# Attention with a gated feed-forward: block 0's row exps in one instruction, a sigmoid by exp and log, and the softmax statistics turned earlier

## The chip, the cores and the metric

The kernel runs on one core of a Trainium2 chip. A core has a matrix engine (TensorE, PE in the profile; PEld is its weight load), a vector engine (VectorE, DVE), a scalar engine for functions like exp (ScalarE, ACT), a general engine (GpSimd, POOL) and a queue for transfers (SyncE, SP). Each engine works through its own list of instructions in order; semaphores make one wait for another. The metric is the device time of the kernel in microseconds (us), the median of several runs.

## The reference

The input x has 16 batches of 512 rows of 128 numbers, all float32. Cut to what matters:

```
xn = layernorm(x)
q, k = xn @ Wq, xn @ Wk          # 16 heads of 8
v = xn @ Wv                      # 16 heads of 64
attn = softmax(causal(q k^T / sqrt(8)))      # 512 x 512 for each head
a = (attn @ v) @ Wo
prev = xn moved down by one row, a row of zeros first
xr, xk = mu_r*xn + (1-mu_r)*prev, mu_k*xn + (1-mu_k)*prev
f = sigmoid(xr @ W_r^T) * (relu(xk @ W_k^T)^2 @ W_v^T)
out = x + a + f
```

## The kernel before

**Two passes over the scores.** For a softmax row one needs its maximum and the sum of its exps. The kernel computes the scores twice. The first pass has queries on the partitions: PE writes them to a PSUM tile `sm` (`rowscores`), adds the causal mask by further small products (`rowmask`), DVE takes each row's negated maximum `negm` (`rowmax`), and ACT takes exps with `negm` as bias and sums them along the row into `z` (`rowsum`). The log of `z` (`log_sums`, ACT) is subtracted from `negm` (`sub_logs`, DVE); the result `lz` is the number that turns a score into the log of its weight. `turn_stats` transposes `lz` on PE (tile `pm`) and DVE splits it into a high and a low part (`mh`, `ml`); `put_stats` sends these by four DMAs, issued by POOL, into two extra rows of the query tile `q`. The second pass has keys on the partitions: `scores` (PE, tile `sT`) multiplies with the extra rows, so that the exp of its result is the finished weight. `weights` (ACT) takes that exp into `e`, POOL zeroes what lies above the diagonal, and `weigh` (PE, tile `av`) multiplies with `v`. `take_ctx` (DVE) copies the sum out as `ctx`, and `project_out` (PE, tile `po`) applies Wo.

**Tiling.** Heads are taken in pairs, one head on partitions 0 to 63 and one on 64 to 127, and two pairs make a group. A row block is 128 queries; block i has (i+1) x 128 keys at or below the diagonal. A group's blocks are packed into five tiles, `ROWS` for the first pass and `KEYS` for the second. A unit handles one tile of each. In `ROWS`, tiles 0 and 2 hold block 2 (384 keys) and block 0 (128 keys) of one pair, tiles 1 and 3 hold block 3 (512), and tile 4 holds block 1 (256) of both pairs. A batch is four groups, so 20 units, and unit n of kind t = n mod 5.

**Order.** The order of the work is written out by hand: `_InOrder` keeps every engine's instructions in the order of the program. `unit_work(n)` issues, for unit n, the first pass's row scores and masks for the tile that is 11 units ahead, the second pass's scores for tile n, any turn of statistics that is due, `take_ctx`, the maxima of the tile 11 ahead, the row exps of the tile 10 ahead (`LEAD`), the weights of tile n, and then the pieces and the weighted values. The pieces are the rest of the work (normalising, projections, the feed-forward part), put into units by `at(n, ...)`; they come before the weighted values, and in units of kind 1 after them. A group's log of sums is taken in a unit of kind 4; `sub_logs` is appended to the pieces of the next unit, the turn comes one unit after that, and the sending one more after.

**Buffers.** `sm` has two buffers of two PSUM banks, `sT` one of two banks, `av` one bank, and one bank `m` is shared by all pieces (`m_tile`), `pm` included. So row scores wait for ACT's row exps two tiles back, and scores wait for the last unit's weights.

**Feed-forward.** `ffn_r` makes the argument of the sigmoid in tile `pr`; DVE copies it with a lower clamp into `e_sig`, ACT takes exp(-x) (`ffn_exp`), POOL adds 1, and DVE's reciprocals in four parts give `sig` (`ffn_sig`). `ffn_out` multiplies with it.

**Transfers.** `project_qk` writes q and k of a later batch to DRAM and `spread_qk` (SP) reads them back in the layout of the pairs, in 16 transfers per batch at written-out units.

Of the kernel before, what the change touches and what calls it, by code (L numbers as in the profile page):

```python
# [17 lines left out]
P = 128  # L18
# [7 lines left out]
LEAD = 10  # L26
EPS = 1e-5
MASKED = -3.0e38
SIG_MIN = -87.5


class _InOrder:
# [15 lines left out]
def attn_ffn_kernel(  # L48
# [119 lines left out]
    def product_turned(out, lhsT, rhs, start=True, stop=True):  # L168


        for t in range(NB):
            for c in range(2):
                first = t * P + 64 * c
                pe.matmul(
                    out[64 * c : 64 * c + 64, t * D : (t + 1) * D], lhsT[:, first : first + 64],
                    rhs, start=(start and t == 0), stop=(stop and t == NB - 1),
                )
# [85 lines left out]
    def ffn_r(b):  # L263
        pr = m_tile(f"pr_{b}")
        product_turned(pr, xmix.pop((b, 0)), ffn_w[:, 0, :])
        e = one.tile([P, T], FP, tag="e_sig", name=f"e_sig_{b}")

        dve.tensor_scalar(e, pr, SIG_MIN, None, ALU.max)
        ffns[b, "e"] = e

    def ffn_exp(b):
        e = ffns[b, "e"]
        act.activation(e, e, AF.Exp, scale=-1.0)
        pool.tensor_scalar(e, e, 1.0, None, ALU.add)

    def ffn_sig(b, c):
        if c == 0:
            ffns[b] = one.tile([P, T], FP, tag="sig", name=f"sig_{b}")
        cols = slice(c * P, (c + 1) * P)
        dve.reciprocal(ffns[b][:, cols], ffns[b, "e"][:, cols])  # L280

    def ffn_k(b):
        pk = m_tile(f"pk_{b}")
# [57 lines left out]
    def rowmask(b, g, t):  # L341

        ends = [to + (i + 1) * P for _, i, to in ROWS[t]]
        step = ends[-1] - ends[0] or P
        for c in range(2):
            for u in range(2):
                s = slice(64 * u, 64 * u + 64)
                cols = sms[b, g, t][:, u, ends[0] - P :]
                if len(ends) > 1 and step > P:
                    cols = cols.rearrange("q (m k) -> q m k", k=P)[:, 0 :: step // P, 64 * c :]  # L350
                else:
                    cols = cols.rearrange("q (m k) -> q m k", k=P)[:, :, 64 * c :]
                pe.matmul(
                    cols, id64[s, c, :],
                    mask64[s, c : c + 1, 64 * c :].to_broadcast([64, len(ends), P - 64 * c]),
                    start=False, stop=(c == 1),
                )

    def rowmax(b, g, t):
        if t == 0:  # L360
            stats[b, g] = (
                stat.tile([P, 2, 2, NB], FP, tag="negm", name=f"negm_{b}_{g}"),
                stat.tile([P, 2, 2, NB], FP, tag="z", name=f"z_{b}_{g}"),
            )
        negm, sm = stats[b, g][0], sms[b, g, t]
        blocks = ROWS[t]
        if len({i for _, i, _ in blocks}) < len(blocks):
            dve.tensor_reduce(
                negm[:, :, :, blocks[0][1]], sm.rearrange("q u (w k) -> q u w k", w=len(blocks)),
                AX.X, ALU.max, negate=True,  # L370
            )
            return
        for w, i, to in blocks:
            dve.tensor_reduce(
                negm[:, :, w, i], sm[:, :, to : to + (i + 1) * P], AX.X, ALU.max, negate=True
            )

    def rowsum(b, g, t):
        negm, z = stats[b, g]
        sm = sms.pop((b, g, t))  # L380
        for w, i, to in ROWS[t]:
            for u in range(2):
                cols = sm[:, u, to : to + (i + 1) * P]
                act.activation(
                    cols, cols, AF.Exp,
                    bias=negm[:, u, w, i : i + 1], accum_out=z[:, u, w, i : i + 1],
                )

    def log_sums(b, g):
        lz = stat.tile([P, 2, 2, NB], FP, tag="lz", name=f"lz_{b}_{g}")  # L390
# [7 lines left out]
    def turn_stats(b, g):  # L398

        lz = stats.pop((b, g))[2]  # L400
        pm = m_tile(f"pm_{b}_{g}")[:, 0:P]
        pe.transpose(pm[0 : 4 * NB], lz.rearrange("q u p i -> q (u p i)"), ident)
        hi = stat.tile([4 * NB, P], FR, tag="mh", name=f"mh_{b}_{g}")
        lo = stat.tile([4 * NB, P], FR, tag="ml", name=f"ml_{b}_{g}")
        dve.tensor_copy(hi, pm[0 : 4 * NB])
        dve.tensor_tensor(lo, pm[0 : 4 * NB], hi.bitcast(FP), ALU.subtract)
        stats[b, g] = (hi, lo)

    def put_stats(b, g):

        for n, half in enumerate(stats.pop((b, g))):
            for u in range(2):
                r = 64 * u + RS + n
                pool.dma_start(
                    out=qs[b % 2].bitcast(FP)[r : r + 1, 2 * g : 2 * g + 2, :].rearrange(
                        "o p (i t) -> o (p i) t", t=P
                    ),
                    in_=half.bitcast(FP)[2 * NB * u : 2 * NB * u + 2 * NB],
                )
# [72 lines left out]
    def at(n, f, *args):  # L492
        todo.setdefault(n, []).append((f, args))
# [4 lines left out]
    for b in range(B):  # L498
        n0 = b * per
        if b + 1 < B:  # L500
            r = 0 if b else 7
            at(n0 + r, ffn_r, b + 1)
            at(n0 + r + 1, ffn_exp, b + 1)
            for c, n in enumerate((3, 8, 13, 18) if b else (11, 13, 14, 18)):
                at(n0 + n, ffn_sig, b + 1, c)
            for m, n in enumerate((1 if b else 3, 5, 12, 13, 14, 16, 17, 18)):
                at(n0 + n, project_v, b + 1, m // 2, m % 2)
            at(n0 + 7, mix_prev, b + 1, 1)
            at(n0 + 9, mix, b + 1, 1)
            at(n0 + 11, ffn_k, b + 1)  # L510
            at(n0 + 19, ffn_out, b + 1)
            for m, n in enumerate((-3, -1, 0, 1, 4, 5, 5, 6) if b else (0, 0, 1, 1, 4, 5, 5, 6)):
                at(n0 + n, spread_qk, b + 1, *SPREAD[m], slice(0, NPAIR // 2))
            for m, n in enumerate((6, 9, 9, 10, 10, 11, 14, 14)):
                at(n0 + n, spread_qk, b + 1, *SPREAD[m], slice(NPAIR // 2, NPAIR))
        if b + 2 < B:
            at(n0 + 4, deviation, b + 2)
            for c in range(NB):
                at(n0 + (1, 1, 3, 3)[c], row_moments, b + 2, c)
                at(n0 + 4 + c // 2, normalise, b + 2, c)  # L520
            at(n0 + 6, transpose_xn, b + 2)
            at(n0 + 10, project_qk, b + 2, False)
            at(n0 + 15, project_qk, b + 2, True)
            at(n0 + 12, mix_prev, b + 2, 0)
            at(n0 + 14, mix, b + 2, 0)
        for p, n in enumerate((2, 3, 3, 4, 7, 8, 8, 9) if b < B - 1 else (-8, -7, -7, -6, -3, -2, 0, 3)):
            at(n0 + per + n, project_out, b, p)
        if b + 3 < B:
            at(n0 + 11, load_x, b + 3)

    def unit_work(n):
        now, stat_now, stat_next = (unit_of(n + m) for m in (0, LEAD, LEAD + 1))
        if n in puts:
            put_stats(*puts.pop(n))
        if stat_next:
            rowscores(*stat_next)
            rowmask(*stat_next)
        if now:
            scores(*now)
        if n in turns:  # L540
            turn_stats(*turns.pop(n))
        t = n % UNITS
        done = {0: (n - UNITS, 0), 2: (n - UNITS, 1)}.get(t)
        if done and unit_of(done[0]):
            b, g, _ = unit_of(done[0])
            take_ctx(b, 2 * g + done[1])
        if stat_next:
            rowmax(*stat_next)

        if stat_now:  # L550
            rowsum(*stat_now)
            b, g, kind = stat_now
            if kind == UNITS - 1:
                log_sums(b, g)
                at(n + 1, sub_logs, b, g)
                turns[n + 2] = puts[n + 3] = b, g
        if now:
            weights(*now)
        pieces = todo.pop(n, ())
        if t != 1:  # L560
            for f, args in pieces:
                f(*args)
        since, w, blocks = WEIGHED[t]
        if unit_of(n - since):
            b, g, _ = unit_of(n - since)
            for j in blocks:
                weigh(b, 2 * g + w, j, (t, j) in ((1, 3), (4, 3)))
        if t == 1:
            for f, args in pieces:
                f(*args)  # L570

    halves = {}

# [74 lines left out]
        at(first - 1 + 5 * i, mix_prev, 0, i)  # L648
        at(first + 1 + 6 * i, mix, 0, i)
    at(first + 8, ffn_r, 0)  # L650
    at(first + 9, ffn_exp, 0)
    for c, n in enumerate((1, 2, 3, 3)):
        at(n, ffn_sig, 0, c)
    at(2, ffn_k, 0)
    at(4, ffn_out, 0)
    at(1, mix_prev, 1, 0)
# [40 lines left out]
```

## Time and profile before

| what | value |
|---|---|
| device time, median of 3 runs | 1035.7 us (1035.53 to 1037.13) |
| the profiled execution's own time | 1035.34 us |
| its span, first to last instruction | 1033.5 us |
| mean granted TensorE clock | 0.976 |
| row exps on ACT (1024), busy | 513.4 us, and 201.3 us of accumulator reads that overlap them in part |
| weights' exps on ACT (320) | 324.5 us, 1014 ns each |
| row maxima on DVE (448) | 397.2 us |
| reciprocals on DVE (64) | 60.2 us, 941 ns each |
| statistics, POOL's DMA issues (256) | 136.8 us |

A line of the timeline gives start, duration, engine, operation, output<-input, shapes and, in brackets, the idle time before it with what ended it. A row of the groups gives busy time, mean ns of one, and idle time before. All rows have the line of the helper (L42), so work is told apart by the names of tiles. In the windows, (x) counts instructions; the last three columns are the granted TensorE clock, the share of the DMA engines, and GB/s.

### The profile page before, as it was taken

The numbers are of one execution on the slowest core, as the hardware profiler recorded it, in microseconds if no ns is written. First come the engines' busy times: TensorE is split into PE (matmuls) and PEld (weight loads), VectorE is DVE, ScalarE is ACT, GpSimd is POOL, SyncE is SP. The second block draws the span as 40 slices with busy tenths as digits, with TensorE's granted clock in tenths as the row PEclk, the third lists the DMA queues.
The fourth block names the chain that finished last, engine by engine and source line by source line (L and its number), as shares of the span: only waits on it lengthen the run. The fifth ranks groups of instructions, "written<-read, shape, count | busy, mean of one in ns | idle before, by whom it ended". The sixth has DMA issues, their size and how long they took to land.

```text
span 1033.5 us, 23971 instructions
## 1 busy us (share of the span) xinstructions
PE 976.3 (94%) x8771; PEld 527.6 (51%) x8771; DVE 793.9 (77%) x1316; ACT 923.9 (89%) x2449; POOL 514.1 (50%) x957
## 2 busy tenths in 40 slices
PE   3789999999999999999999999999999999999997
PEld 1344464555546455554645555464554646455454
DVE  4787879688887878787797877878787797877741
ACT  0788999899999999999899999999999999999982
POOL 4165454544646464463645545564464546444432
PEclk8778999999999999999999999999999999999999
DMA  7722515034250512525043252504324150432000
GB/s 193 136 28 49 99 34 112 15 73 84 59 98 19 114 29 73 85 59 98 3 108 50 58 100 50 97 14 107 50 58 90 34 102 4 110 37 48 3 12 11
DMA packets 59971, 67.17 MB, mean 65 GB/s; under 512 B 12928, under 2 KB 33024, under 8 KB 59856
## 3 DMA queue, kind: packets, MB, share of 16 engines
q1 hardware_dynamic: 48688, 61.89, 30.8%
q0 software_dynamic: 8640, 1.34, 1.1%
q10 hardware_dynamic: 2528, 2.43, 0.9%
q8 instruction: 70, 1.15, 0.5%
q14 instruction: 45, 0.37, 0.2%
HBM read 39.13 MB, written 25.17 MB: 62 GB/s over the span
## 4 chain that ended last, share of the span: by engine, by line
PE 49%; ACT 32%; DVE 11%; issue 4%; DMA 3%; POOL 1%; POOLq 0%; ACTq 0%
ACT sm L42 22%; PE av L42 14%; ACT e L42 10%; PE po L42 10%; PE sm L42 8%; PE sT L42 7%; DVE negm L42 6%; DMA q<-ml 3%; PE pv L42 3%; PE pq L42 2%; PE pk L42 2%; PE pr L42 1%; PE pm L42 1%; DVE mh L42 1%; DVE ml L42 1%
## 5 line engine op out<-in xcount | busy, mean ns | idle before, releaser
L42 ACT ACTIVATE sm<-sm,negm 128x384 f32<-128x384 f32 (+3 forms) x1024 | 513.4, 501 | 78.1 <-DVE negm L42 29.3
L42 DVE TENSOR_REDUCE negm<-sm 128x2 f32<-128x768 f32 (+3 forms) x448 | 397.2, 909 | 77.8 <-PE sm L42 77.8
L42 POOL TENSOR_SCALAR_AFFINE_SELECT e<-e 128x256 f32<-128x256 f32 x512 | 203.5, 416 | 457.1 <-ACT e L42 454.5
L42 ACT ACTIVATE e<-sT 128x1024 f32<-128x1024 f32 x320 | 324.5, 1014 | 18.5 <-PE sT L42 18.2
L42 PE MATMUL av<-e,v 128*64 128x512 f32 (+3 forms) x2048 | 338.3, 441 | 1.1 <-DVE ctx L42 0.5
L42 PEld LDWEIGHTS av<-e,v 128*64 128x64 f32 x2048 | 138.7, 138 | 166.5 <-issue 130.7
L42 ACT ACTIVATION_READ_ACCUMULATOR sm<-sm,negm 128x1 f32 x1024 | 201.3, 197 | 0.0
L42 PE MATMUL sT<-q,k 35*128 35x512 f32 (+3 forms) x1024 | 164.0, 366 | 23.5 <-ACT e L42 13.9
L42 PE MATMUL sm<-k,q 33*128 33x384 f32 (+3 forms) x1024 | 164.0, 378 | 8.3 <-ACT sm L42 8.3
L42 PEld LDWEIGHTS sm<-k,q 33*128 33x128 f32 x1024 | 83.1, 188 | 169.0 <-ACT sm L42 89.3
L42 PE MATMUL pv<-wv,xnT 128*64 128x512 f32 x512 | 139.0, 622 | 1.5 <-DVE ffn L42 0.9
L42 PE MATMUL po<-wo,ctx 128*64 128x128 f32 x2048 | 133.2, 277 | 1.6 <-DVE ctx L42 1.6
L42 PEld LDWEIGHTS po<-wo,ctx 128*64 128x64 f32 x2048 | 109.8, 137 | 18.6 <-issue 7.8
L42 PEld LDWEIGHTS sT<-q,k 35*128 35x128 f32 x1024 | 86.6, 189 | 49.0 <-ACT e L42 36.8
L42 PE MATMUL sm<-mask,id 64*128 64x128 bf16 (+2 forms) x1280 | 101.0, 236 | 0.0
L42 DVE COPY ctx<-av 128x512 f32<-128x512 f32 x128 | 87.3, 682 | 16.0 <-PE av L42 15.9
L42 DVE COPY v<-pv 128x512 f32<-128x512 f32 x128 | 86.0, 672 | 4.3 <-PE pv L42 0.6
L42 DVE CAST mh<-pm 16x128 fp32r<-16x128 f32 x64 | 17.8, 278 | 79.3 <-PE pm L42 79.3
L42 POOL DMA_DIRECT2D q<-mh x128 | 70.7, 555 | 12.9 <-DVE mh L42 7.6
L42 POOL DMA_DIRECT2D q<-ml x128 | 66.1, 521 | 0.0
L42 DVE RECIPROCAL sig<-e_sig 128x128 f32<-128x128 f32 x64 | 60.2, 941 | 0.0
L42 POOL TENSOR_SCALAR prev<-xnT,omm 128x512 f32<-128x512 f32 x32 | 50.2, 1567 | 14.0 <-DVE xmix L42 14.0
(65 smaller groups left out, 599.4 us busy)
## 6 DMA issues: line engine op xcount, KB each, us to landing
q<-q SPq DMA_DIRECT2D x124, 128.0 KB, 4.8
k<-k SPq DMA_DIRECT2D x124, 128.0 KB, 5.1
k<-kh SPq DMA_DIRECT2D x30, 256.0 KB, 2.6
x<-in_L_attn_x_dram SPq DMA_DIRECT2D x16, 256.0 KB, 2.9
q<-qh SPq DMA_DIRECT2D x16, 256.0 KB, 4.2
q<-ql SPq DMA_DIRECT2D x16, 256.0 KB, 4.3
out_dram<-o SPq DMA_DIRECT2D x16, 256.0 KB, 2.8
k<-kl SPq DMA_DIRECT2D x15, 256.0 KB, 2.0
```

The source lines that it names most:

```text
L42: return self._tc.keep_in_program_order(f(*args, **kwargs))
```

## The change

1. **Row exps of block 0.** In tiles 0 and 2, DVE adds `negm` to block 0's scores of both heads in place, after the two maxima. ACT then takes the exp of both heads' block 0 (128 x 256) in one instruction, without bias and without a sum, into an SBUF tile `first`; it stands between the two exps of block 2. DVE sums `first` into `z` one unit later (`sum_first`).
2. **Sigmoid.** DVE writes low = min(r, 0) and e = r - 2 low, which is |r|; ACT takes exp(-e) and log(1 + that); POOL subtracts it from low; five units later ACT's exp gives the sigmoid. The reciprocals and the clamp are gone.
3. **Masks.** `rowmask` comes after `scores` in a unit instead of before.
4. **Turn.** `turn_stats` comes one unit earlier, as the last thing of its unit, and `put_stats` one unit earlier.
5. **Spreads.** Units of the 16 `spread_qk` transfers are moved by up to two units.

```diff
     def ffn_r(b):
...
-        dve.tensor_scalar(e, pr, SIG_MIN, None, ALU.max)
-        ffns[b, "e"] = e
-
-    def ffn_exp(b):
-        e = ffns[b, "e"]
+        low = one.tile([P, T], FP, tag="low", name=f"low_{b}")
+        dve.tensor_scalar(low, pr, 0.0, None, ALU.min)
+        dve.scalar_tensor_tensor(e, low, -2.0, pr, ALU.mult, ALU.add)
+        ffns[b, "e"] = e, low
+
+    def ffn_log(b):
+        e, low = ffns[b, "e"]
         act.activation(e, e, AF.Exp, scale=-1.0)
-        pool.tensor_scalar(e, e, 1.0, None, ALU.add)
-
-    def ffn_sig(b, c):
-        if c == 0:
-            ffns[b] = one.tile([P, T], FP, tag="sig", name=f"sig_{b}")
-        cols = slice(c * P, (c + 1) * P)
-        dve.reciprocal(ffns[b][:, cols], ffns[b, "e"][:, cols])
+        act.activation(e, e, AF.Ln, bias=1.0)
+        pool.tensor_tensor(low, low, e, ALU.subtract)
+
+    def ffn_sig(b):
+        ffns[b] = one.tile([P, T], FP, tag="sig", name=f"sig_{b}")
+        act.activation(ffns[b], ffns.pop((b, "e"))[1], AF.Exp)
...
         for w, i, to in blocks:
-            dve.tensor_reduce(
-                negm[:, :, w, i], sm[:, :, to : to + (i + 1) * P], AX.X, ALU.max, negate=True
-            )
+            cols = sm[:, :, to : to + (i + 1) * P]
+            dve.tensor_reduce(negm[:, :, w, i], cols, AX.X, ALU.max, negate=True)
+            if i == 0:
+                dve.tensor_tensor(
+                    cols, cols, negm[:, :, w, i : i + 1].to_broadcast([P, 2, P]), ALU.add
+                )
+
+    def sum_first(first, z):
+        dve.tensor_reduce(z, first, AX.X, ALU.add)
...
-        for w, i, to in ROWS[t]:
+        for w, i, to in (x for x in ROWS[t] if x[1]):
             for u in range(2):
...
+                for v, k, to_k in ROWS[t]:
+                    if k == 0 and u == 0:
+                        first = small.tile([P, 2, P], FP, tag="first", name=f"first_{b}_{g}_{v}")
+                        act.activation(first, sm[:, :, to_k : to_k + P], AF.Exp)
+                        at(now + 1, sum_first, first, z[:, :, v, k])
...
-            at(n0 + r + 1, ffn_exp, b + 1)
-            for c, n in enumerate((3, 8, 13, 18) if b else (11, 13, 14, 18)):
-                at(n0 + n, ffn_sig, b + 1, c)
+            at(n0 + r + 1, ffn_log, b + 1)
+            at(n0 + r + 6, ffn_sig, b + 1)
...
-            for m, n in enumerate((-3, -1, 0, 1, 4, 5, 5, 6) if b else (0, 0, 1, 1, 4, 5, 5, 6)):
+            for m, n in enumerate((-1, -1, 0, 0, 4, 4, 5, 5) if b else (0, 0, 0, 0, 4, 4, 5, 5)):
...
-            for m, n in enumerate((6, 9, 9, 10, 10, 11, 14, 14)):
+            for m, n in enumerate((8, 9, 9, 10, 10, 14, 14, 15)):
...
         if stat_next:
             rowscores(*stat_next)
-            rowmask(*stat_next)
         if now:
             scores(*now)
-        if n in turns:
-            turn_stats(*turns.pop(n))
+        if stat_next:
+            rowmask(*stat_next)
...
-                turns[n + 2] = puts[n + 3] = b, g
+                turns[n + 1] = puts[n + 2] = b, g
...
+        if n in turns:
+            turn_stats(*turns.pop(n))
```

More of the change, by code (lines that the diff above doesn't have):

```diff
@@ L28 @@
 MASKED = -3.0e38
-SIG_MIN = -87.5
 class _InOrder:
@@ L373, in rowmax, with rowsum @@
         for w, i, to in blocks:
-            dve.tensor_reduce(
-                negm[:, :, w, i], sm[:, :, to : to + (i + 1) * P], AX.X, ALU.max, negate=True
-            )
-    def rowsum(b, g, t):
+            cols = sm[:, :, to : to + (i + 1) * P]
[6 more added lines that the diff above has]
+        dve.tensor_reduce(z, first, AX.X, ALU.add)
+    def rowsum(now, b, g, t):
         negm, z = stats[b, g]
         sm = sms.pop((b, g, t))
-        for w, i, to in ROWS[t]:
+        for w, i, to in (x for x in ROWS[t] if x[1]):
             for u in range(2):
@@ L550, in unit_work @@
         if stat_now:
-            rowsum(*stat_now)
+            rowsum(n, *stat_now)
             b, g, kind = stat_now
@@ L650, in attn_ffn_kernel @@
     at(first + 8, ffn_r, 0)
-    at(first + 9, ffn_exp, 0)
-    for c, n in enumerate((1, 2, 3, 3)):
-        at(n, ffn_sig, 0, c)
+    at(first + 9, ffn_log, 0)
+    at(1, ffn_sig, 0)
     at(2, ffn_k, 0)
```

## The prediction

> **What bounds the kernel now.** I read the busy shares first, then the waits, then windows over one batch, then the timeline of single units. Times are us from the span's start; t0 to t4 are the five kinds of unit (unit number mod 5).
>
> The page, with its groups (busy, mean ns, idle before) and the list of waits (total us, times, longest):
>
> ```profile
> PE 976.3 (94%) x8771; PEld 527.6 (51%) x8771; DVE 793.9 (77%) x1316; ACT 923.9 (89%) x2449; POOL 514.1 (50%) x957
> L42 ACT ACTIVATION_READ_ACCUMULATOR sm<-sm,negm 128x1 f32 x1024 | 201.3, 197 | 0.0
> L42 ACT ACTIVATE sm<-sm,negm 128x128 f32<-128x128 f32 x256 | 87.6, 342 | 8.3
> DVE mh L42 <- PE pm L42: 79.3, 64, 3.2
> ACT sm L42 <- DVE negm L42: 29.3, 60, 2.1
> PE sT L42 <- DMA q<-ml: 4.5, 4, 2.0
> ```
>
> Windows over the four groups (five units each) of one batch, columns as named in the page, PE, PEld, DVE, ACT, POOL:
>
> ```profile
> 547.84:562.89 15.05, 14.56 (x165) 9.35 (x165) 10.83 (x19) 14.66 (x40) 7.94 (x14) 1.00 0.24 40
> 562.89:577.97 15.08, 15.02 (x161) 9.20 (x157) 11.09 (x22) 14.26 (x40) 10.98 (x19) 1.00 0.01 2
> 577.97:593.04 15.07, 15.07 (x117) 6.73 (x111) 13.99 (x23) 14.24 (x39) 7.95 (x14) 1.00 0.46 98
> 593.04:608.00 14.96, 14.45 (x121) 7.01 (x119) 13.04 (x20) 14.23 (x39) 5.17 (x12) 1.00 0.72 137
> ```
>
> A batch is 60.16 us; PE and ACT both have almost no idle time, and in the last two groups DVE has 14.0 and 13.0 of 15. DVE, PE and ACT therefore form one loop. Its turn is the timeline at t0 and t1 of the third group (DVE, then PE, then ACT):
>
> ```profile
> 576.71 1.29 DVE L42 TENSOR_REDUCE negm<-sm 128x2 f32<-128x768 f32 x2 [1.42 <-PE sm L42]
> 578.03 0.69 DVE L42 TENSOR_TENSOR o<-po,y 128x512 f32<-128x512 f32 x1
> 578.64 0.74 DVE L42 SCALAR_TENSOR_TENSOR xmix<-xnT,mus,prev 128x512 f32<-128x512 f32 x1
> 579.30 0.69 DVE L42 COPY ctx<-av 128x512 f32<-128x512 f32 x1
> 579.90 1.22 DVE L42 TENSOR_REDUCE negm<-sm 128x2 f32<-128x1024 f32 x1
> 581.03 0.68 DVE L42 CAST qh<-pq 128x512 fp32r<-128x512 f32 x1
> 581.75 0.69 DVE L42 TENSOR_TENSOR ql<-pq,qh 128x512 fp32r<-128x512 f32 x1
> 582.36 0.28 DVE L42 TENSOR_TENSOR lz<-negm,lz 128x16 f32<-128x16 f32 x1
> 581.92 0.50 PE L42 MATMUL sm<-k,q 33*128 33x384 f32 x4
> 582.83 0.28 PE L42 MATMUL pm<-ident,lz 128*16 128x128 f32 x1
> 584.97 0.56 ACT L42 ACTIVATE sm<-sm,negm 128x384 f32<-128x384 f32 x1 [0.44 <-DVE negm L42]
> ```
>
> DVE runs without a gap from 576.71 to 582.64 and lz is its last item. PE has reached the end of t0 (the start of t1's row scores) at 581.92, 0.72 before lz ends. Today that costs nothing: pm comes after scores, at 582.83. In the four groups lz ends 0.40 before, 0.31 before, 0.72 after and 0.33 after that PE moment.
>
> [...] In the built program the first row exp of t0 and t2 waits for DVE's count after the new addition, which touches the same banks. [...]
>
> **The change part by part**, start to start in the timeline unless said.
>
> 1. Row exps of block 0. ACT loses 4 exps of 128 per group, 0.49 each with their accumulator reads (565.20 to 566.05 is two), and gains 2 of 256 without accumulator: 0.37 by the row of the 1024-wide e (1014 ns less 768 at 0.83), 0.42 with its hand-over. t0 and t2 fall from 2.25 to 1.69: 0.56 twice per group. DVE gains an addition in place at t4 and t1 (0.43, 0.45 with hand-over; bounds 0.35 and 0.6, as no row writes PSUM from DVE) and a 256-wide sum at t1 and t3 (0.41 busy by the row 128x2<-128x256, 0.35 net; bounds 0.30 and 0.41). The addition stands between the maxima and ACT's first row exp, so it is wholly on that path: the maxima's 1.27 become 1.74.
>
> 2. Masks behind both scores: masks, hence maxima, come 0.42 later where PE is the late one; turned scores 0.1 to 0.15 earlier.
>
> 3. Sigmoid. DVE loses 4 reciprocals of 0.94 per batch, all at t3 (3, 8, 13, 18), where it waits for masks anyway: worth almost nothing. It gains one 512-wide operation (0.61) at t0 of the first group, ahead of lz. ACT gains Ln (0.65) and Exp (0.52) in t1 units, where it will wait for maxima: hidden, 1.2 per batch if not. POOL's addition of 1494 ns becomes a subtraction (1269 by the ffn row), hidden.
>
> 4. Turn. pm moves from after t1's scores to PE's end of t0; DVE loses mh and ml (0.54) from in front of t1's maxima. But pm now waits for lz, and behind it on PE stand t1's row scores, scores and masks, for which DVE's maxima and then ACT wait. mh, ml then run under those scores.
>
> 5. Statistics (four POOL DMAs of about 0.53) leave a unit earlier. POOL now waits at t1's start for mh and ml, with t1's selections queued behind the issues; their values are weighed two units later, so this is hidden, and would cost PE about 1 per group otherwise. Spreads of the next q and k (SP) start at -1 instead of -3, so they no longer share the engines with group 0's statistics. The waits at batch starts (4.5, and 1.8 at 179.5 named ACT) and the lower clock after them made two batches 3.0 and 3.4 longer than 60.2 (products at 144.65, 207.87 and 434.86, 498.47, spaced 63.2 and 63.6) and others 0.3 to 0.9: about 8 us, which I count as won. Nearest new collision: k's DRAM writes at unit 15 ahead of statistics at 16, needed 4 units later; the typical landing is 1.7 us.
>
> **The sum.** I walked the loop by hand: PE row scores 0.35, masks 0.10 or 0.15, scores 0.42 (not before the last weights' start + 1.07), a piece 0.91 to 0.93, weighted values 1.39, 1.01, 0.96, 0.52, 0.96 for t0 to t4, pm 0.21; maxima 0.38 after masks begin; ACT 0.04 after maxima; weights 0.91. For the kernel before, this gives weights of t4 15.06 and 30.16 after 547.84; the trace has 15.05 and 30.13.
>
> Third group after, from t4's weights (577.97 in before): maxima and addition end at 1.0, o, xmix, ctx end at 2.8, t1's maximum 3.95, qh, ql 5.3, lz 5.45. PE is ready for pm at 4.1 and waits 1.35. Row scores 5.7, scores 6.05, masks 6.45, maxima 6.85 to 8.55, ACT at t2 8.6; before, 584.97 - 577.97 = 7.0. From there ACT saves 0.56 in t2 and loses 0.25 to t3's maximum (ctx and the sum delay it). Group: 15.07 + 1.6 - 0.56 + 0.25 = 16.4.
>
> First group after, from t4's weights: scores 1.05, pr's product ends 2.5, weighted values 3.9. DVE: maximum 1.8 to 2.95, low 3.55, e 4.15, lz 4.35, so pm waits 0.45 to 4.35; row scores 4.55, scores 4.9, masks 5.35, maxima and addition 5.7 to 7.45. ACT: t1's weights cannot start before 5.45 (scores + 0.53), then Exp and Ln 1.2, t2 at 7.55 (before: 7.0, without the Ln). DVE goes on with v 8.1, st 8.5, the sum 8.85, ctx 9.45, and t3's maximum ends at 10.65 where ACT was ready at 10.15. Group 15.6.
>
> The others: second 15.0 (pm hardly waits), fourth 15.5 (pm waits 0.7 behind kh, kl, and the addition at t4). Batch 62.5 against 60.2, +2.3; allowing one more wait of av for ctx, 2.4.
>
> Thirteen full batches: +31. First batch and lead-in (DVE-bound at 60 to 80: 18.73 of 20): +2.5. Last two batches lose most pieces, lz is early and ACT's saving shows (about 1 in each of five groups, less some loss): -3. Statistics: -8. Sum +22.5 on the profiled 1033.5 span (1035.3 with 1.8 around it, 0.4 under the median of 1035.7): about 1057.
>
> **Rivals.** (a) Relief, the other side: lz meets PE in time. Then a group is E(t4) to scores 1.07, 2.6 to 2.7 of PE at t0 with pm, row scores and scores 0.77, 0.38, 1.78, ACT 7.5 to the next t4: about 14.5, and PE's own sum is 58.1 a batch. 14 x 1.8 + 8 + 5 = 38 less: 997. It decides at a lz lead of zero; against it, lz is already 0.72 late in one group before anything is added. For it: ACT has no other gap, and the 29.3 us of waits on maxima are partly mh and ml. (b) Partial: the DVE chain absorbs half of my delay (+1.1 a batch less 8 and 3, plus lead-in): about 1040; with a little more, even. (c) Worse: the addition costs 0.6 and adds 0.17 twice per group: +11 to 15, 1070. (d) The statistics still land late: +8, 1065.
>
> **Chances.** Likeliest 0.57, (c) and (d) 0.10, (b) 0.18 of which a third each slower, equal and faster, (a) and what lies between 0.15. So slower 0.73, same 0.06 (within 0.2%, about what this kernel's measurement can tell), faster 0.21. Range 1027 to 1074, from a part of the faster cases to the worse bound; the slower case alone has 1043 to 1070.
>
> **What would show it.** Right: PE waits before pm for DVE's lz, some 0.4 to 1.4 us in three groups of four; ACT's waits on maxima above 29.3 although ACT's busy time falls by some 70 us; DVE near 850; no sT wait on q<-ml; batches of 62 to 63. Wrong: pm without a wait, PE's idle unchanged, batches under 60; or maxima with addition well away from 1.74.

## The result

The changed kernel takes 1062.72 us (median of 4 runs, 1061.54 to 1064.12); the kernel before, in the same comparison, 1035.62 (1033.52 to 1037.13). The ratio is 1.0253, with a 95% interval of 1.0236 to 1.0269: slower by 27 us, where 21 had been forecast (1057 against 1035.7). The profiled execution took 1061.54, with a span of 1059.8 at a mean granted clock of 0.985 (0.976 before), so the clock is no part of the loss.

From the kernel before (rows L42) and after (L41): busy shares, the chain that ended last, and, from the list of waits, total us, times and longest.

```profile
PE 961.8 (91%) x8771; PEld 519.0 (49%) x8771; DVE 844.8 (80%) x1524; ACT 889.3 (84%) x2097; POOL 513.3 (48%) x957
PE 49%; ACT 32%; DVE 11%; issue 4%; DMA 3%; POOL 1%; POOLq 0%; ACTq 0%
PE 43%; DVE 35%; ACT 12%; issue 8%; POOL 1%; DMA 1%; SPq 0%; DVEq 0%; ACTq 0%; POOLq 0%
...
ACT e L42 <- PE sT L42: 18.2, 15, 2.4
ACT e L41 <- PE sT L41: 49.7, 65, 1.8
PE pm L41 <- DVE lz L41: 39.2, 57, 1.5
ACT sm L41 <- DVE sm L41: 36.6, 19, 25.7
DVE mh L41 <- PE pm L41: 30.6, 64, 1.8
ACT sm L41 <- PE pk L41: 17.0, 16, 1.7
ACT sm L41 <- PE pv L41: 14.6, 15, 1.0
ACT sm L41 <- DVE negm L41: 12.9, 32, 1.8
```

In the chain (before first, then after), DVE has gone from 11% to 35% and ACT from 32% to 12%. PE's wait ahead of pm was 1.1 us in all before; it is now 39.2, in 57 of 64 groups. DVE's wait for pm, 79.3 before, is 30.6. The wait of sT on q<-ml (second-pass scores waiting for the statistics that were sent), 4.5 before, is gone.

ACT does less and idles more. Its busy time falls by 34.6 (923.9 to 889.3), while its time without work rises from 109.6 to 170.5 (span less busy), by 60.9; the difference is the 26.3 by which the span grew. Two waits make up nearly all of that rise. ACT's wait for sT grew from 18.2 to 49.7, that is 31.5. Its wait ahead of row exps was 29.3, all under the name negm; now it goes mainly under four names, because the first row exp waits for DVE's addition and for PE: 36.6 less the 25.7 of the program's start, 17.0, 14.6 and 12.9, so 55.4, or 26.1 more (two small entries, 2.7 and 0.7, left out).

Windows over the four groups of one batch (columns PE, PEld, DVE, ACT, POOL, each with its count; clock, DMA share, GB/s):

```profile
544.57:560.10 15.53, 14.38 (x122) 7.01 (x117) 13.85 (x24) 13.40 (x34) 5.51 (x12) 1.00 0.62 130
560.10:575.81 15.71, 14.49 (x166) 9.17 (x162) 12.05 (x23) 14.43 (x35) 7.69 (x14) 1.00 0.28 45
575.81:591.30 15.49, 14.92 (x163) 9.21 (x161) 11.84 (x25) 14.03 (x34) 11.01 (x19) 1.00 0.01 2
591.30:607.74 16.44, 15.09 (x117) 6.68 (x113) 14.44 (x25) 13.62 (x33) 7.82 (x14) 1.00 0.39 82
```

The edges are the starts of t4's weights, as in the prediction's table; the first row answers its fourth. The groups that the prediction called first to fourth take 15.71, 15.49, 16.44 and 15.53. PE, at 14.45 to 15.07 busy of about 15 before, now has 0.6 to 1.35 without work in every group.

The third group's turn, t0 and t1, from the timeline (DVE, then PE, then ACT; in brackets the idle time before):

```profile
590.50 1.29 DVE L41 TENSOR_REDUCE negm<-sm 128x2 f32<-128x768 f32 x2 [1.68 <-PE sm L41]
591.90 0.43 DVE L41 TENSOR_TENSOR sm<-sm,negm 128x256 f32<-128x256 f32 x1
592.24 0.68 DVE L41 TENSOR_TENSOR o<-po,y 128x512 f32<-128x512 f32 x1
...
596.05 0.69 DVE L41 TENSOR_TENSOR ql<-pq,qh 128x512 fp32r<-128x512 f32 x1
596.66 0.16 DVE L41 TENSOR_TENSOR lz<-negm,lz 128x16 f32<-128x16 f32 x1
594.43 1.51 PE L41 MATMUL av<-e,v 128*64 128x512 f32 x8 [0.31 <-DVE ctx L41]
596.97 0.27 PE L41 MATMUL pm<-ident,lz 128*16 128x128 f32 x1 [1.02 <-DVE lz L41]
598.05 1.02 ACT L41 ACTIVATE e<-sT 128x1024 f32<-128x1024 f32 x1 [1.01 <-PE sT L41]
600.10 0.56 ACT L41 ACTIVATE sm<-sm,negm 128x384 f32<-128x384 f32 x1 [1.02 <-PE pk L41]
```

This is the loop that was forecast. PE stands still at pm for 1.02 us, and had already stood 0.31 for ctx. Scores come late behind it, ACT's t1 weights wait 1.01 for them, and its t2 row exps wait 1.02 more. They start 8.80 after t4's weights (591.30); before, it was 7.00.

A ledger of the difference can be read off the spacing of every fourth pm, that is one batch. Before, an undisturbed batch took 60.2, and the 13 batches between the first and the last summed to 792.6, which is 10.0 above 13 x 60.2: batches of 63.2 and 63.6 and smaller excesses. In these two the granted clock was 0.50 from 182 to 185 us and from 489 to 492, shortly after waits of PE that ended at 181.30 (1.80 long) and 486.76 (1.96), and 0.97 over the batch. All of the excess sits in the first group of a batch: from one log of z to the next that group takes 15.05 to 18.4, while each of the other three repeats within 0.05. The waits on q<-ml stand there, and the kernels without such waits show no excess in it, so I put the 10.0 down to late statistics. After, they took 63.1 or 63.2 (63.7 once) and summed to 821.5.

| term | forecast | measured |
|---|---|---|
| 13 batches, slower loop | +31 | 821.5 - 782.6 = +38.9 |
| late statistics gone | -8 | -10.0 |
| lead-in, first batch, tail | +2.5 - 3 | -2.6 (64.0 for 65.1, 59.5 for 60.3, rest -0.7) |
| span | +22.5, written as 1057 | +26.3 |

### The profile page after: what moved, and what is told of

It reads as the page before. It is cut to its first block, busy times and chain, and to the rows that moved or that the text cites. A ratio compares the mean times of both kernels' runs of the same rounds, so it can differ in the third digit from the quotient of the medians.

```text
span 1059.8 us, 24148 instructions
## 1 busy us (share of the span) xinstructions
PE 961.8 (91%) x8771; PEld 519.0 (49%) x8771; DVE 844.8 (80%) x1524; ACT 889.3 (84%) x2097; POOL 513.3 (48%) x957
## 3 DMA queue, kind: packets, MB, share of 16 engines
q1 hardware_dynamic: 48688, 61.89, 30.6%
## 4 chain that ended last, share of the span: by engine, by line
PE 43%; DVE 35%; ACT 12%; issue 8%; POOL 1%; DMA 1%; SPq 0%; DVEq 0%; ACTq 0%; POOLq 0%
DVE negm L41 14%; PE av L41 11%; PE sm L41 10%; PE po L41 8%; ACT sm L41 7%; PE sT L41 6%; PE pv L41 5%; ACT e L41 4%; DVE ctx L41 4%; DVE v L41 4%; DVE sm L41 2%; PE pm L41 2%; PE pk L41 2%; DVE xmix L41 1%; DVE z L41 1%
## 5 line engine op out<-in xcount | busy, mean ns | idle before, releaser
L41 ACT ACTIVATE sm<-sm,negm 128x384 f32<-128x384 f32 (+2 forms) x768 | 425.8, 554 | 102.5 <-DVE sm L41 36.6
L41 DVE TENSOR_REDUCE negm<-sm 128x2 f32<-128x768 f32 (+3 forms) x448 | 399.3, 916 | 123.9 <-PE sm L41 123.9
L41 POOL TENSOR_SCALAR_AFFINE_SELECT e<-e 128x256 f32<-128x256 f32 x512 | 203.5, 417 | 407.9 <-ACT e L41 406.9
L41 ACT ACTIVATE e<-sT 128x1024 f32<-128x1024 f32 x320 | 324.8, 1015 | 50.4 <-PE sT L41 49.7
L41 PE MATMUL av<-e,v 128*64 128x512 f32 (+3 forms) x2048 | 338.5, 440 | 10.7 <-DVE ctx L41 10.2
L41 PEld LDWEIGHTS av<-e,v 128*64 128x64 f32 x2048 | 134.2, 136 | 190.7 <-issue 171.4
L41 PE MATMUL sm<-k,q 33*128 33x384 f32 (+3 forms) x1024 | 163.3, 376 | 6.3 <-ACT sm L41 6.3
L41 PE MATMUL sT<-q,k 35*128 35x512 f32 (+3 forms) x1024 | 143.1, 331 | 15.6 <-ACT e L41 15.5
L41 PEld LDWEIGHTS sm<-k,q 33*128 33x128 f32 x1024 | 82.6, 186 | 149.9 <-ACT e L41 63.9
L41 ACT ACTIVATION_READ_ACCUMULATOR sm<-sm,negm 128x1 f32 x768 | 150.1, 195 | 0.0
L41 PE MATMUL pv<-wv,xnT 128*64 128x512 f32 x512 | 138.7, 620 | 2.0 <-DVE e_sig L41 1.3
L41 PE MATMUL po<-wo,ctx 128*64 128x128 f32 x2048 | 133.2, 277 | 3.8 <-DVE ctx L41 1.6
L41 PEld LDWEIGHTS po<-wo,ctx 128*64 128x64 f32 x2048 | 109.8, 137 | 18.7 <-issue 9.7
L41 POOL DMA_DIRECT2D q<-mh x128 | 70.2, 552 | 87.8 <-DVE mh L41 83.2
L41 PEld LDWEIGHTS sT<-q,k 35*128 35x128 f32 x1024 | 90.0, 187 | 34.8 <-ACT e L41 30.2
L41 PE MATMUL sm<-mask,id 64*128 64x128 bf16 (+2 forms) x1280 | 102.9, 235 | 0.0
L41 DVE COPY ctx<-av 128x512 f32<-128x512 f32 x128 | 87.2, 681 | 12.8 <-PE av L41 12.7
L41 DVE COPY v<-pv 128x512 f32<-128x512 f32 x128 | 87.5, 683 | 1.5
L41 DVE TENSOR_TENSOR sm<-sm,negm 128x256 f32<-128x256 f32 x128 | 55.4, 432 | 13.6 <-ACT lz L41 0.5
L41 POOL DMA_DIRECT2D q<-ml x128 | 66.1, 521 | 0.0
L41 POOL TENSOR_SCALAR prev<-xnT,omm 128x512 f32<-128x512 f32 x32 | 50.1, 1566 | 13.9 <-DVE xmix L41 13.9
L41 PEld LDWEIGHTS <-id 64*128 64x128 bf16 x1280 | 40.4, 97 | 29.6 <-issue 17.2
```

The costliest lines, as they stand in the source:

```text
L41: return self._tc.keep_in_program_order(f(*args, **kwargs))
```

## The experiments

Each run compares with runs of the kernel before on the same chip, whose median there lay between 1037.4 and 1039.4. "Batch" is the spacing of every fourth pm in an undisturbed batch, one whose statistics came in time; against 60.2 before and 63.1 after.

| run | ratio (95%) | median us | batch | PE's wait ahead of pm, us |
|---|---|---|---|---|
| after, lz first | 1.0232 (1.0200 to 1.0265) | 1062.55 | 63.1 | 30.2 |
| after, turn back | 1.0118 (1.0086 to 1.0150) | 1050.99 | 62.0 | none |
| after, masks ahead | 1.0073 (1.0052 to 1.0095) | 1045.61 | 62.0 | 35.3 |
| after, old row exps | 1.0076 (1.0042 to 1.0110) | 1046.69 | 61.9 | 29.0 |
| before + row exps | 1.0081 (1.0059 to 1.0102) | 1044.55 | 61.6 | 1.1 |
| before + sigmoid | 1.0063 (1.0042 to 1.0083) | 1042.24 | 60.8 | 0.3 |
| before + masks behind | 1.0064 (1.0043 to 1.0084) | 1045.53 | 60.8 | 1.2 |
| before + turn | 0.9842 (0.9820 to 0.9863) | 1019.65 | 59.8 | 19.6 |
| before + turn + masks | 0.9943 (0.9926 to 0.9960) | 1032.87 | 60.8 | 24.1 |
| before + spreads | 1.0006 (0.9987 to 1.0025) | 1038.89 | 60.2 | 1.1 |
| after with a common maximum | 0.9998 (0.9972 to 1.0024) | 1037.76 | 59.5 | none |
| before + turn + common maximum | 0.9941 (0.9915 to 0.9967) | 1033.10 | 61.1 | 21.0 |

### What pm waits for

My reading of the trace was that lz is late. The test takes lz out of its place behind the pieces and makes it DVE's first item in its unit.

```diff
         t = n % UNITS
+        if n in subs:
+            sub_logs(*subs.pop(n))
...
-                at(n + 1, sub_logs, b, g)
+                subs[n + 1] = b, g
```

> The changed kernel with one thing moved: the subtraction that makes lz is the first thing DVE does in its unit, ahead of ctx, the maximum and the piece. Theory L (PE stands before pm because lz is late in DVE's queue): PE's waits before pm fall from 39.2 us to under 10, and the time to about 1035 to 1045. Rival B (pm also needs the one PSUM bank m that all pieces share, so it waits for DVE's last read of the piece of that unit, which stands just before lz in DVE's queue today): pm waits only 0.15 us less each, the waits stay at 25 us or more under the name of ql, kl, e_sig or v, and the time stays at 1052 to 1060.

From its list of waits, and pm in a third and a fourth group from its timeline:

```profile
PE pm L41 <- DVE ql L41: 12.3, 13, 0.9
PE pm L41 <- DVE kl L41: 12.2, 14, 0.9
...
597.49 0.27 PE L41 MATMUL pm<-ident,lz 128*16 128x128 f32 x1 [0.94 <-DVE ql L41]
550.06 0.27 PE L41 MATMUL pm<-ident,lz 128*16 128x128 f32 x1 [0.90 <-DVE kl L41]
```

The rival's mechanism holds, though the time, 1062.55, lies above its range too. lz is early now, and pm still waits 0.94 and 0.90, for ql and kl: DVE's last reads of the piece's tile. Pieces and pm share one buffer, the bank `m`, and pm takes the same columns. So pm has two conditions, lz and the buffer, and the profile names the one that comes last. In the third group they are 0.08 apart (1.02 to 0.94). Moving lz alone gave 0.0 per batch, but as a sum: the second group became 0.18 shorter and the fourth, where lz now delays the piece, 0.21 longer. A buffer of its own for pm was not tried.

### Undoing one part of the change

The turn (with the sending) back to its old place, behind scores and masks of the next unit:

```diff
+        if n in turns:
+            turn_stats(*turns.pop(n))
...
-                turns[n + 1] = puts[n + 2] = b, g
+                turns[n + 2] = puts[n + 3] = b, g
...
-        if n in turns:
-            turn_stats(*turns.pop(n))
```

> The changed kernel with the turn back in the next unit, behind its scores and masks, and the sending one unit later again; all else as changed. Theory (the place of pm is the main loss): PE's waits before pm nearly vanish, but mh and ml stand again in front of t1's maxima, which now also carry the addition, so part of the gain is given back: 1045 to 1055. Rival M (the addition on the path of the maxima is the main loss, not the turn): within 5 us of the changed kernel, 1058 to 1068. Whether group 0's statistics come late again is seen in the waits of sT on q<-ml: none expected, as the spreads keep their new units.

Masks ahead of scores again:

```diff
             rowscores(*stat_next)
+            rowmask(*stat_next)
         if now:
             scores(*now)
-        if stat_next:
-            rowmask(*stat_next)
```

> The changed kernel with the masks ahead of the scores again. Theory (DVE's chain of maxima, addition, piece, lz is what PE waits for): each maximum starts some 0.3 to 0.4 us earlier where PE is the late one, 0.3 to 0.5 us per group: 1035 to 1048. Rival (the order of masks and scores does not matter, since PE has both within 0.7 us anyway): within 5 us of the changed kernel.

The row exps of before (block 0 by head, bias and sum in the exp, no addition, no `sum_first`):

```diff
-            if i == 0:
-                dve.tensor_tensor(
-                    cols, cols, negm[:, :, w, i : i + 1].to_broadcast([P, 2, P]), ALU.add
-                )
...
-        for w, i, to in (x for x in ROWS[t] if x[1]):
+        for w, i, to in ROWS[t]:
```

> The changed kernel with the row exps of block 0 as before: no addition and no sum on DVE, four exps of 128 with accumulator reads on ACT. Theory (addition and sum cost more on DVE's chain than they save on ACT): ACT's busy time rises by about 90 us, DVE's falls by about 108, and the time falls to 1035 to 1048. Rival A (ACT's saving is what keeps the loss small): it rises to 1065 to 1080.

All three fell into the theory's ranges: 1050.99, 1045.61 and 1046.69. Each part, taken out of the whole, gives back 1.1 to 1.3 us per batch. With the turn back, pm no longer appears among PE's waits on lz, and DVE waits 51.5 for pm instead of 30.6. The page of the kernel with the old row exps:

```profile
PE 961.5 (92%) x8771; PEld 526.2 (50%) x8771; DVE 750.4 (72%) x1268; ACT 944.4 (90%) x2481; POOL 515.5 (49%) x957
```

ACT has 55.1 us more work than the changed kernel, and the kernel is faster: what counts is on DVE's side, which has 94.4 less. (About 90 and 108 had been expected.) Even so pm waits 29.0 there.

### One part alone

The row exps alone on the kernel before (the same edit as in the change's diff):

```diff
+            if i == 0:
+                dve.tensor_tensor(
+                    cols, cols, negm[:, :, w, i : i + 1].to_broadcast([P, 2, P]), ALU.add
+                )
...
+                        act.activation(first, sm[:, :, to_k : to_k + P], AF.Exp)
+                        at(now + 1, sum_first, first, z[:, :, v, k])
```

> The kernel before with the row exps of block 0 alone changed. Theory (the addition of 0.47 stands on the path from masks to ACT and takes back what ACT saves in the same tile, 0.56, and the sum on DVE delays t3's maximum): ACT's busy time falls by about 90 us and the time stays at 1030 to 1045. Rival A (ACT is the bound, so its saving shows): 1000 to 1020.

```profile
PE 972.6 (93%) x8771; PEld 521.1 (50%) x8771; DVE 870.3 (83%) x1572; ACT 864.0 (83%) x2065; POOL 522.2 (50%) x957
...
ACT sm L42 <- DVE sm L42: 117.4, 66, 26.0
```

ACT loses 59.9 us of work and waits for it: 117.4 less the start's 26.0, plus 11.4 on negm, is 102.8 ahead of row exps where it was 29.3. Waits for sT fall by 4.3 (18.2 to 13.9). -59.9 + 73.5 - 4.3 is +9.3; the span grew by 9.6 (1043.1). The time, 1044.55, is inside the theory's range, at its upper end: what ACT saves is lost again, and more. After the first batch no statistics are late in this run, so the loop's price, 13 x 1.4 = 18, is half hidden by the 10 that it wins back. Whether the addition or the sum costs more was not run.

The sigmoid alone:

```diff
-        pool.tensor_scalar(e, e, 1.0, None, ALU.add)
...
-        dve.reciprocal(ffns[b][:, cols], ffns[b, "e"][:, cols])
+        act.activation(e, e, AF.Ln, bias=1.0)
+        pool.tensor_tensor(low, low, e, ALU.subtract)
...
+        act.activation(ffns[b], ffns.pop((b, "e"))[1], AF.Exp)
```

> The kernel before with the sigmoid alone changed. Theory (the reciprocals stood where DVE waits for masks, while Ln stands in a unit in which ACT has no gap): 0.65 us more per batch, the second Exp hidden in the ACT gap before t2: 1042 to 1050. Rival D (DVE's 49 us fewer show): 1020 to 1033.

1042.24, at the theory's edge: DVE's work falls by 34.7 (793.9 to 759.2) and ACT's rises by 15.1 (923.9 to 939.0). A batch grows by 0.6, about the length of one Ln (the 32 exps and logs on `e_sig` take 626 ns each in the kernel after). All of it falls into the first group, where the Ln stands (15.05 to 15.69); the second, which gets the last exp, is as before (15.11 and 15.07). What DVE saves buys nothing here.

The masks alone, with the same lines as above in the other direction:

> The kernel before with the masks alone behind the scores. Theory (masks behind cost only where the turn at the unit's end, or the addition, makes DVE's chain the path): within 4 us of the kernel before, 1033 to 1041. Rival (masks behind cost some 15 us by themselves, as undoing them in the changed kernel gave): 1045 to 1055.

1045.53 against 1039.36 on the same chip: the theory (1033 to 1041) is wrong. Undisturbed batches take 60.8 (+0.6), and DVE's idle time before the row maxima (negm waiting for sm) is 133.0 in the list of waits, where the kernel before has 77.8. Statistics still come late (sT on q<-ml 4.2 in all).

The turn alone (the edit of the second diff above, reversed):

> The kernel before with the turn alone at the end of its unit, and the sending a unit earlier. Theory (the turn's new place costs only because DVE is late there, from masks behind scores, addition and second sigmoid operation; without these the piece's reads and lz end about when PE arrives): PE waits before pm under 10 us in total, ACT's 29 us of waits on maxima mostly vanish as mh and ml leave the path, and the statistics come in time: 1008 to 1022. Rival T (the place itself costs, since pm must wait for DVE): PE's waits before pm above 25 us and 1040 or more.

```profile
PE pm L42 <- DVE lz L42: 19.6, 30, 2.0
...
ACT sm L42 <- DVE negm L42: 4.7, 5, 1.4
...
553.42:567.93 14.51, 14.51 (x158) 8.96 (x153) 10.94 (x22) 14.12 (x39) 10.95 (x19) 1.00 0.01 2
567.93:583.34 15.41, 14.65 (x115) 6.73 (x113) 13.62 (x22) 14.40 (x40) 8.26 (x14) 1.00 0.45 96
```

**This one beats both kernels**, at 1019.65, 1.6% under the kernel before. The time fits the theory; the waits do not: 19.6 for pm lies between its "under 10" and the rival's "above 25". PE waits 0.67 and 0.50 in the third and fourth group and not at all in the others, close to the leads of lz that the prediction had read in the kernel before (0.72 and 0.33 late, the others early). ACT's wait for maxima is almost gone (29.3 to 4.7), since mh and ml no longer stand in front of them (at t1 of the third group before, mh, ml and the maxima start one behind the other at 583.15, 583.46 and 583.67; the masks had begun at 582.27). The two windows are the second and third group of one batch: without a wait the second takes 14.51 for 15.08, the third 15.41 for 15.07. Every batch takes 59.8. Of the 16.2 by which the span falls (1033.5 to 1017.3), the 13 batches give 14.8: 4 to 5 the loop, 10 the late statistics. The last batch gives 2.8 (57.5 for 60.3), of which the first and the end give back 1.3.

So the turn's sign depends on what stands around it: alone it wins 0.3 to 0.4 a batch, in the whole it costs 1.1. The next run puts back one of the neighbours, the masks:

```diff
             rowscores(*stat_next)
-            rowmask(*stat_next)
         if now:
             scores(*now)
-        if n in turns:
-            turn_stats(*turns.pop(n))
+        if stat_next:
+            rowmask(*stat_next)
...
-                turns[n + 2] = puts[n + 3] = b, g
+                turns[n + 1] = puts[n + 2] = b, g
...
+        if n in turns:
+            turn_stats(*turns.pop(n))
```

> The kernel before with the turn at the unit's end and the masks behind the scores, nothing else. Theory (the two work against each other: the maximum of t4 is later, and with it what DVE does up to lz, for which PE now waits): PE's waits before pm rise from the 19.6 us of the turn alone to over 28, and some 1.4 us per batch are lost against it: 1033 to 1043. Rival (they add up, and masks alone cost nothing): 1017 to 1024.

1032.87, a hair under the theory's range, with pm waiting 24.1 instead of the more than 28 that were expected. The masks add 1.0 a batch on top of the turn (0.6 to 0.7 alone). Read the other way: beside the masks the turn no longer shortens the loop (60.8 with and without it), and the 12.7 us between the two runs (1045.53 and 1032.87) are mostly the late statistics that it removes (9.4 above 13 undisturbed batches in the masks alone). From there to the loss of 1.1 in the whole only the row exps, the sigmoid and the spreads are left; DVE's added work is in the row exps. That it is this work was not run as a pair with the turn.

Group by group the turn's sign goes with PE's wait. In its three comparisons (alone, beside the masks, in the whole against the run with the turn back), groups in which pm waits 0.41 or less change by -0.60 to -0.02, those with a wait of about 0.5 by -0.09 to +0.20, and those with 0.67 to 1.02 by +0.33 to +0.54. The turn pays where lz is ready and costs where PE stands for it.

### The spreads

Most of these transfers move by at most two units; one moves by three (11 to 14).

```diff
-            for m, n in enumerate((-3, -1, 0, 1, 4, 5, 5, 6) if b else (0, 0, 1, 1, 4, 5, 5, 6)):
+            for m, n in enumerate((-1, -1, 0, 0, 4, 4, 5, 5) if b else (0, 0, 0, 0, 4, 4, 5, 5)):
...
-            for m, n in enumerate((6, 9, 9, 10, 10, 11, 14, 14)):
+            for m, n in enumerate((8, 9, 9, 10, 10, 14, 14, 15)):
```

> The kernel before with the units of the spreads alone moved. Theory (group 0's statistics came late because the spreads at -3 shared the DMA engines with them): the waits of sT on q<-ml vanish and the time is 1025 to 1031. Rival (the statistics are late because they are sent late, whatever the spreads do): waits of sT on q<-ml stay at 4 us or more, 1033 to 1040.

```profile
PE sT L42 <- DMA q<-ml: 10.1, 9, 2.4
```

The rival holds: with the spreads moved and nothing else, statistics are as late as before (10.1 where the profile of before has 4.5), batches reach 63.0, and the time stays. What does cure them is open in part. After the first batch they are gone in each of the six runs that send a unit earlier (among them the turn alone, with the old spreads), and also in two that send at the old place in a slower loop. The seven kernels that send at the old place fall in order of their undisturbed batch: sT waits 13.4 on q<-ml at 59.5, 10.1 and 4.5 at 60.2, 6.2 and 4.2 at 60.8 (sigmoid alone, masks alone), 0.5 at 61.6 (row exps alone) and nothing at 62.0 (turn back). So either an earlier sending or a slower loop goes with statistics in time. That the pace is the cause was not tried by itself, and no run sent earlier without turning earlier.

### A version without the addition

If the addition is what hurts, block 0 of both heads can share one maximum. That makes the maximum the bias of one exp, and the softmax is the same in exact arithmetic; a copy gives the second head its `negm`. Masks and turn were put back to their old places.

```diff
+            if i:
+                dve.tensor_reduce(negm[:, :, w, i], cols, AX.X, ALU.max, negate=True)
+            else:
+                dve.tensor_reduce(negm[:, 0:1, w, i], cols, AX.XY, ALU.max, negate=True)
+                pool.tensor_copy(negm[:, 1:2, w, i], negm[:, 0:1, w, i])
...
+                            first, sm[:, :, to_k : to_k + P], AF.Exp, bias=negm[:, 0, v, k : k + 1]
```

> The changed kernel with masks ahead, the turn back in the next unit, and without the addition: block 0 of both heads takes one common maximum (a reduction over both heads, copied to the second head by POOL), so that one exp with that bias serves both; the sums per head stay on DVE. The softmax is the same in exact arithmetic. Theory (of the change to the row exps, the addition on the path is what costs): ACT keeps its saving, maxima are as in the kernel before: 1005 to 1022. Rival S (the sums and the second sigmoid operation on DVE cost as much): 1030 to 1045.

```profile
PE sT L41 <- DMA q<-ml: 13.4, 12, 1.9
```

1037.76, spread from 1032 to 1047: the rival's time, but not for its reason. An undisturbed batch is 59.5, the fastest loop of all runs; most batches are not undisturbed (up to 64.7), since statistics land late 12 times here. The sigmoid alone takes 60.8, and the spreads change a batch by at most 0.1, so by difference block 0's exps in this form are worth about 1.2 a batch, where the form with the addition costs 1.4. For the loop this supports the theory that the addition is what costs. POOL, which issues their DMAs, also stands 289.4 us in front of the small copies. Whether that queue or the faster loop makes them late was not tried on its own.

The obvious next step was the turn alone with the common maximum, the copy on DVE:

```diff
+    def sum_first(first, z, low):
+        dve.tensor_reduce(z, first, AX.X, ALU.add)
+        dve.tensor_copy(low[:, 1:2], low[:, 0:1])
...
-                turns[n + 2] = puts[n + 3] = b, g
+                turns[n + 1] = puts[n + 2] = b, g
```

> The kernel before with the turn at the unit's end, and block 0's row exps of both heads in one instruction with one common maximum (a reduction over both heads; DVE copies it to the second head beside the sum, a unit later), so no addition in place; masks, sigmoid and spreads as before. Theory (ACT's saving of 0.47 twice per group shows where the path runs through ACT, until PE's own work of about 14.5 us per group is the bound): 1000 to 1013. Rival (PE and DVE are already the bound with the turn alone, 14.9 us per group): 1014 to 1022.

1033.10: both ranges missed, above the rival's 1022. Every batch takes 61.1, 1.3 more than with the turn alone, although ACT has 46.1 us less to do (877.2). DVE has 40.1 more (837.7), and ACT's wait on negm is back at 50.4. So beside the turn, a saving on ACT paid for with DVE work loses in this form too. Against the run before it, four things differ: the turn, the reciprocals that stay on DVE, the copy on DVE, and the spreads. Which of them, or of the sum and the copy, does it was not separated.

## Why the prediction was right, and where it was not

The sign, the range and the mechanism held: DVE, PE and ACT form one loop, in which DVE's added work sits ahead of PE's turn while ACT's saving turns into waiting. Most signs named at its end came out: PE waits for pm of 0.50, 0.41, 1.02 and 0.71 in the four groups (0.45, hardly, 1.35, 0.7 were walked; in the third, 0.31 for ctx comes ahead of the 1.02), so in all four groups and not in three; waits for maxima of 55.4; DVE at 844.8; no wait on q<-ml. Two were off. The batch, 63.1, is just above "62 to 63". ACT's busy time fell by 34.6 and not some 70. The durations of ACT's instructions, added up over its groups, did fall by 69.4 (1064.4 to 995.0). Busy time counts an overlap once, and ACT's instructions overlapped by 140.5 in all before and by 105.7 after: 384 row-exp instructions that each overlapped their neighbours are gone, and ACT has more gaps.

**The batch** was walked as 62.5, or 62.6 with the wait for ctx, and is 63.1: the mis-sized term, +38.9 against +31. The total missed by less than this term: the statistics gave 2 more than counted, and the lead-in and first batch came out 1.3 shorter where +2.5 had been put (the end gave only about half of its 3). That these errors offset each other is luck. The recorded sum also gives 1035.7 + 22.5 = 1058.2, not the "about 1057" written there. By groups the walk gave 15.6, 15.0, 16.4, 15.5 and the trace 15.71, 15.49, 16.44, 15.53. So nearly all of the miss is in the second group, where "pm hardly waits" was 0.41.

**Step 1, row exps.** Costed as a DVE addition of 0.43 to 0.47 wholly on ACT's path, and right in kind. The groups by form give the addition's own duration and those of its partners (busy, mean ns, then idle before):

```profile
L41 DVE TENSOR_TENSOR sm<-sm,negm 128x256 f32<-128x256 f32 x128 | 55.4, 432 | 13.6 <-ACT lz L41 0.5
L41 DVE TENSOR_REDUCE z<-first 128x2 f32<-128x256 f32 x128 | 52.4, 409 | 0.0
L41 ACT ACTIVATE first<-sm 128x256 f32<-128x256 f32 x128 | 49.2, 384 | 4.0
```

432 ns stands against the 0.43 that was put in as the author's estimate. A straight line through two rows of before (ml 278 ns at 128 wide, ql 691 at 512) gives, as an estimate too, 416. The 0.37 and 0.41 also fit (384 and 409 ns); the 0.83 ns an element behind the 0.37 is the slope of the row exps of before (342 ns at 128 wide, 662 at 512). But from the maxima's start to their hand-over it is 1.83 (598.17 to 600.00), not 1.74: the addition needs the maximum just taken and starts 0.11 after its end. The price at the head of ACT's path is 0.56, close to the 0.6 that rival (c) had assumed. Alone, this step costs 1.4 a batch.

**Step 2, masks** was treated as a shift of 0.42 where PE is late, with no price of its own in the sum. Alone it costs 0.6 to 0.7 a batch, and in the whole 1.1. My expectation before the run of masks alone repeated the error.

**Step 3, sigmoid.** That the reciprocals are worth nothing is confirmed. "1.2 per batch if not hidden" was the bound for Ln and Exp; alone 0.6 shows, about one of the two.

**Step 4, turn.** The wait and the queue behind it were right, its ground only half: "pm waits for lz" names the last of two conditions. In the third group bank m comes free only 0.1 earlier, and an earlier lz was worth nothing over the batch. That the turn in itself is a gain here, and a loss only beside the others, was not in the prediction.

**Step 5, statistics.** The 8 came out as 10, for another cause than the one named: not the spreads. Of the rivals, (a) relief did not come true for the whole. Its mechanism is real: with the turn alone the second group, where lz is in time, takes 14.51, and (a) had worked out 14.5. (d) is excluded by the missing wait on q<-ml.

The parts alone add up to 2.2 to 2.4 a batch (1.4 for the row exps, 0.6 each for masks and sigmoid, less 0.4 for the turn, rounded); the whole costs 2.9 to 3.0. In time the gap is wider (0.81 + 0.63 + 0.64 + 0.06 - 1.58 = +0.56% by single ratios, +2.53% in the whole): 0.6 to 0.7 x 13, 8 to 9 us, are the interplay in the loop, and row exps and turn each remove the late statistics' 10 us, which can be removed only once. Together 18 to 19, of a gap of 20.

## What to carry to other kernels

When three engines hand each other work in a loop, add up the loop through every engine before trading work from one to another: 60 us less on ACT were lost to 73 us of new waiting when the replacement stood between ACT's producer and ACT; without the addition, and with the copy on POOL, the loop became shorter (59.5 a batch). Test the parts of a bundled change singly: here one of five was worth 1.6% alone (about a quarter of it the loop, the rest mostly statistics in time) and was buried under the rest, and its sign changed with its neighbours. When an instruction waits for the last of several conditions, move that one and look at what is named next before building on it.

## What was not expected of the hardware

- In the kernel after, DVE instructions that need the result of the one before start after its end: the addition 0.11 us after the maxima (591.79 to 591.90 and 599.46 to 599.57), ql 0.04 after qh (596.01 to 596.05). One that doesn't, o, starts 0.09 before (592.24, the addition's end at 592.33). Between the two the difference in start is 0.13 to 0.2.
- The 256-wide exp into `first` took 475 ns in the run with the common maximum, where it takes its bias from a tile, one number per partition, and 384 in the kernel after, where it has no bias: 91 more.
- Whether the small statistics transfers landed in time went with the pace of the loop: sent at the old place they are late with undisturbed batches of 59.5 to 60.8, in time at 61.6 and 62.0, and in time at 59.8 when sent a unit earlier. Moving the large transfers alone changed nothing (1.0006).
